# A mixture-of-experts layer after an attention: gates worked out chunk by chunk during the attention, tokens gathered without their layernorm, first expert weights fetched early

## The chip, the cores and the metric

The kernel runs on one core of a Trainium2 chip, as one launch. The metric is the device time in microseconds, taken as the median of several runs. Five engines work side by side, each through its own queue of instructions in order: TensorE (PE, with its weight loads shown as PEld), VectorE (DVE), ScalarE (ACT), GpSimd (POOL) and SyncE (SP), which only issues the transfers. They wait for each other through semaphores.

## What is computed

The input is two images of 56 x 56 tokens (L = 3136) with 128 channels. Four layers follow one another: two state-space layers with convolutions, one layer of attention and a long-convolution mixer, and a last layer of attention and experts. The change lies in the last layer:

```python
t = t + _L3_attn_ref(_ln_t(t), ...)      # softmax attention over all 3136 tokens, per image
t = t + _L3_ffn_ref(_ln_t(t), ...)       # experts

def _ln_t(v, eps=1e-5):                  # per token, over its 128 channels
    return (v - mean(v)) / sqrt(var(v) + eps)

def _L3_ffn_ref(x, gate_w, gate_b, weight1, weight2):     # E = 64 experts, K = 8
    logits = x @ gate_w.T + gate_b                         # [b, 3136, 64]
    probs = softmax(logits, axis=1)                        # over the tokens
    vals, idx = top_k(probs.transpose(0, 2, 1), K)         # each expert takes its 8 best tokens
    pooled[b, e] = sum_k vals[b, e, k] * x[b, idx[b, e, k]]
    h = gelu(pooled[b, e] @ weight1[e, :128] + weight1[e, 128])
    o = h @ weight2[e, :512] + weight2[e, 512]
    out[b, idx[b, e, k]] += vals[b, e, k] * o[b, e]
```

All arithmetic that matters here is in fp32. Each expert has 128 x 512 and 512 x 128 weights, 0.5 MB together, 33.5 MB for 64 experts, which are read from DRAM once.

## The kernel before

The kernel is written in a tile framework: pools give out buffers in on-chip memory, the framework derives waits from who reads and writes which buffer, and a scheduler lays each engine's instructions in an order that may differ a little from the order in the program.

**Tokens.** `k.X` holds the residual stream, [112, 28, 2, 128]: 28 tiles of 112 tokens, two images, 128 channels. Seven chunks (NCH) of 448 tokens make up an image.

**Attention 3** (`Attention3.run`, `Attend.run`). Keys of the first image are prepared, then 14 chunks of 448 queries run, seven per image. In each, 25 steps j go over 128 keys: a product `sc` on PE (L1031), Exp on ACT (L1033), a running sum `total` on POOL (L1042, L1044), and, two steps later, the product `av` (L1025). Beside that, up to j = 15 of every chunk but the last, `Queries.some` forms a bound for the next chunk's scores: two bf16 products `lo` a step (L966) and a maximum of each on DVE (L970). `lo` has two banks of PSUM, `sc` three, `pr` one. At the end of a chunk the result is normalised and added to X (L1060 to L1070). A hook `also(at, j)` is called after each step; in chunks 0 to 3 it prepares the second image's keys: at j = 1 and 13 `tokens` (four transposes L1202, sum into X L1203, layernorm), at j = 6 and 18 `channels` (four transposes L1216), at j = 9 and 21 `key_tiles` (L1227). The layernorm of a chunk (`layernorm_tokens`) is L77, L78, L79 on DVE, the squares L80 on ACT, their sum L81 on DVE, the square root L82 on ACT, its reciprocal L83 on DVE and the multiplication L84 on POOL. Square root and Exp need different function tables on ACT, so each layernorm brings two ACT_TABLE_LOADs.

**Experts** (`layer3_experts`, after attention 3 has ended and its memory is free). First SP issues the loads of the gate's weights and of the first four groups of experts (a group is four experts: 1 MB of `w1` and four pieces of 256 KB of `w2`, whose rows in one partition are 512 bytes long). Then:

- layernorm of all tokens, in four pieces of 14 x 128 columns (L79 to L84), into U
- transposes of U to `uT` (L108, 56 of them, copies L64 and L68), then the gates `pr` [128, 3136], with 64 experts of image 0 above 64 of image 1: two accumulated products per chunk (L1695), bias on ACT (L1699)
- softmax over the 3136 columns and the top 8: L1701 to L1709, each over the whole of `pr`. `sel` is then the probability where it is among the top 8, else 0
- `sel` is transposed to tokens (L1714) and each image's 28 tiles of U are multiplied by it, so that `pooled` holds the weighted sums (`pp`, L1719; copies L1724)
- the loop over 16 groups: `ph` (L1747) multiplies `pooled` by `w1` for four experts; a copy, four transposes `pt` (L1758), the bias `b1` and Gelu follow; `every` (L1738) multiplies by `w2` of the group before. A group's buffers are refilled as they come free; `w1` and `w2` are separate tiles, four of each
- `oe` times `sel` gives the output's addition (L1787), X is added (L1792), and the result is stored

Of the kernel before, what the change touches and what calls it, by code (L numbers as in the profile page):

```python
# [70 lines left out]
def layernorm_tokens(k, out, x, sq, st, d):  # L71


    nc = k.nc
    g = x.shape[1]
    mean, var = st[:, 0, :], st[:, 1, :]
    nc.vector.tensor_reduce(mean, x, AX.X, ALU.add)  # L77
    nc.vector.tensor_scalar_mul(mean, mean, 1.0 / d)  # L78
    nc.vector.tensor_tensor(out, x, mean.unsqueeze(2).to_broadcast([TP, g, d]), ALU.subtract)  # L79
    nc.scalar.activation(sq, out, AF.Square)  # L80
    nc.vector.tensor_reduce(var, sq, AX.X, ALU.add)  # L81
    nc.scalar.activation(var, var, AF.Sqrt, bias=k.eps[:TP], scale=1.0 / d)  # L82
    nc.vector.reciprocal(var, var)  # L83
    nc.gpsimd.tensor_tensor(out, out, var.unsqueeze(2).to_broadcast([TP, g, d]), ALU.mult)  # L84


def layernorm_all(k, U):

    with k.tc.tile_pool(name="lnp", bufs=2) as pool:
        for j in range(0, NT, 7):  # L90
            sq = pool.tile([TP, 14, C], F32, name="sq")
            st = pool.tile([TP, 2, 14], F32, name="st")
            layernorm_tokens(
                k,
                U[:, j : j + 7, :, 0:C].rearrange("p j b c -> p (j b) c"),
                k.X[:, j : j + 7].rearrange("p j b c -> p (j b) c"),
                sq, st, C,
            )
# [1024 lines left out]
class Attention3:  # L1123
# [35 lines left out]
    def run(self, A):  # L1159

        k = self.k
        with ExitStack() as ctx:
            kp = ctx.enter_context(k.pool("a3"))
            self.uT = [kp.tile([128, L], F32, name=f"u{b}") for b in range(B)]
            self.low = [kp.tile([128, L], BF16, name=f"low{b}") for b in range(B)]
            self.V = [kp.tile([KT, NKT, C], F32, name=f"V{b}") for b in range(B)]
# [13 lines left out]
            def also(at, j):  # L1180

                half, part = divmod(j, 12)
# [10 lines left out]
            att.run(self.uT, queries, self.V, 1.0 / 16, self.Wv, also=also)  # L1193

# [463 lines left out]
def layer3_experts(k, d, out):  # L1658
# [5 lines left out]
    nc, tc, X = k.nc, k.tc, k.X  # L1664
    NE, NH, EC = 64, 512, 4
    with ExitStack() as ctx:
        sp = ctx.enter_context(tc.tile_pool(name="e3", bufs=1))
        W = {n: load(nc, sp, d["L3_" + n], "L3" + n) for n in ("gate_w", "gate_b", "b1", "b2")}
        wp = ctx.enter_context(tc.tile_pool(name="e3w", bufs=4))
        weights = {}  # L1670

        def fetch(e0):
            w1 = wp.tile([128, EC, NH], F32, name="w1")
            w2 = wp.tile([128, EC, 4, C], F32, name="w2")
            nc.sync.dma_start(w1, d["L3_weight1"][e0 : e0 + EC, 0:C].rearrange("e d h -> d e h"))
            for e in range(EC):
                nc.sync.dma_start(w2[:, e], d["L3_weight2"][e0 + e, 0:NH].rearrange("(c p) o -> p c o", p=128))
            weights[e0] = w1, w2

        for e0 in range(0, 4 * EC, EC):  # L1680
            fetch(e0)
        pr = sp.tile([128, L], F32, name="pr")
        sel = sp.tile([128, L], F32, name="sel")
        pooled = sp.tile([128, NE, 2 * EC], F32, name="pooled")
        nc.gpsimd.memset(pooled, 0.0)
        with tc.tile_pool(name="e3u", bufs=1) as up, tc.tile_pool(name="pe3", bufs=2, space=PSUM) as pp:
            U = up.tile([TP, NT, B, C], F32, name="U")
            layernorm_all(k, U)
            uT = up.tile([128, B, L], F32, name="uT")
            for b in range(B):  # L1690
                tokens_to_channels(k, pp, lambda c0: uT[:, b, c0 : c0 + CH], lambda j: U[:, j, b, :])
            for c in range(NCH):
                ps = pp.tile([128, CH], F32, name="pt")
                for b in range(B):
                    nc.tensor.matmul(  # L1695
                        ps, lhsT=W["gate_w"][:, b, :], rhs=uT[:, b, CH * c : CH * (c + 1)],
                        start=b == 0, stop=b == 1,
                    )
                nc.scalar.activation(pr[:, CH * c : CH * (c + 1)], ps, AF.Identity, bias=W["gate_b"])  # L1699
            m = sp.tile([128, 8], F32, name="m")  # L1700
            nc.vector.tensor_reduce(m[:, 0:1], pr, AX.X, ALU.max, negate=True)  # L1701
            nc.scalar.activation(pr, pr, AF.Exp, bias=m[:, 0:1])
            nc.vector.tensor_reduce(m[:, 1:2], pr, AX.X, ALU.add)
            nc.vector.reciprocal(m[:, 1:2], m[:, 1:2])
            nc.vector.tensor_scalar(pr, pr, m[:, 1:2], None, ALU.mult)
            top = sp.tile([128, 8], F32, name="top")
            nc.vector.max(top, pr)
            nc.vector.match_replace(sel, top, pr, -1.0)
            nc.vector.scalar_tensor_tensor(sel, sel, 0.0, pr, ALU.is_lt, ALU.mult)  # L1709
            selT = up.tile([TP, NT, 128], F32, name="selT")  # L1710
            for j in range(0, NT, 4):
                ps = pp.tile([TP, 4, 128], F32, name="ps")
                for i in range(4):
                    nc.tensor.transpose(ps[:, i, :], sel[:, TP * (j + i) : TP * (j + i + 1)], k.ident)  # L1714
                k.evacuate(selT[:, j : j + 4, :], ps)
            for b in range(B):
                ps = pp.tile([128, NE], F32, name="pp")
                for j in range(NT):
                    nc.tensor.matmul(  # L1719
                        ps, lhsT=U[:, j, b, :], rhs=selT[:, j, NE * b : NE * (b + 1)],  # L1720
                        start=j == 0, stop=j == NT - 1,
                    )
                for e in range(EC):
                    nc.vector.tensor_copy(pooled[:, e::EC, 2 * e + b], ps[:, e::EC])  # L1724
        with tc.tile_pool(name="e3h", bufs=2) as hp, tc.tile_pool(name="pex", bufs=2, space=PSUM) as pp, tc.tile_pool(
            name="poe", bufs=1, space=PSUM
        ) as po:
# [3 lines left out]
            every = po.tile([128, C], F32, name="every")  # L1731
            ready = None

            def second(e0, w2, t):
                for e in range(EC):
                    z = NE - 1 - (e0 + e)
                    for c in range(4):
                        nc.tensor.matmul(  # L1738
                            every, lhsT=t[:, e, c, z : z + 128], rhs=w2[:, e, c, :],
# [3 lines left out]
            for e0 in range(0, NE, EC):  # L1743
                w1, w2 = weights.pop(e0)
                ph = pp.tile([2 * EC, NH], F32, name="ph")
                for e in range(EC):
                    nc.tensor.matmul(  # L1747
                        ph, lhsT=pooled[:, e0 + e, :], rhs=w1[:, e, :], start=e == 0, stop=e == EC - 1
                    )
                hr = hp.tile([2 * EC, NH], F32, name="hr")  # L1750
                nc.vector.tensor_copy(hr, ph)
                if ready is not None:
                    second(*ready)
                    if ready[0] + 4 * EC < NE:
                        fetch(ready[0] + 4 * EC)
                pt = pp.tile([128, 4, EC, B], F32, name="pt")
                for c in range(4):
                    nc.tensor.transpose(  # L1758
                        pt[:, c].rearrange("p e b -> p (e b)"), hr[:, 128 * c : 128 * (c + 1)],
                        k.ident[: 2 * EC, : 2 * EC],  # L1760
# [169 lines left out]
```

## Time and profile before

| what | us |
|---|---|
| median of 5 runs | 9354.45 (9341.42 to 9356.66) |
| profiled execution | 9343.85 |
| its span, first to last instruction | 9341.7 |
| attention 3, of the span | about 8370 to 9100 |
| experts, of the span | about 9100 to 9341.7 |

Busy over the whole span: PE 8138.4 (87%), DVE 7101.5 (76%), POOL 6327.4 (68%), ACT 3856.2 (41%). The granted PE clock is 0.949 in the mean.

A row of the profile that groups instructions names the line, the engine, the operation and the tiles (out<-in), then the count, and its busy time or the mean time of one. The chain of work that ended last is followed back from the end, from each instruction to what released it; "issue" is time for which the profile shows no cause. Rows that begin with numbers are times in us from the start of the span. PE's products in fp32 take two passes, so each appears twice.

### The profile page before, as it was taken

What the parts mean: (1) busy time and instruction counts of PE and PEld (TensorE: products, weight loads), DVE (VectorE), ACT (ScalarE), POOL (GpSimd) and SP (SyncE); (2) the same over time, 40 slices, a digit from 0 to 9 for tenths busy, and PEclk for the clock granted to TensorE, in tenths of its full rate; (3) what the DMA queues carried; (4) which work ended last, traced back from release to release, by engine and by line L of the source; (5) the groups of instructions that cost most, each with busy time, mean ns of one, the idle gap of its engine ahead of it and who ended that gap; (6) DMA issues with size and microseconds to landing.
All of it is one profiled execution on the core that took longest, in us unless ns stands there. A gap on an engine that the chain in (4) does not pass through costs nothing.

```text
span 9341.7 us, 94244 instructions
## 1 busy us (share of the span) xinstructions
PE 8138.4 (87%) x28823; PEld 4793.0 (51%) x28823; DVE 7101.5 (76%) x7517; ACT 3856.2 (41%) x6560; POOL 6327.4 (68%) x4013
## 2 busy tenths in 40 slices
PE   7888888888888888888888888599999999999997
PEld 3444445444444444444444444355588888875545
DVE  8999998999996997998899799711366766665432
ACT  4555545555545555555555555333211111114331
POOL 5999996999994996998899699666411111115550
PEclk9999999999998998999999899699999999999998
DMA  5666664666663884886687488200233333310005
GB/s 155 221 221 214 215 205 132 221 221 214 213 213 95 224 216 122 221 218 166 179 222 214 124 221 215 71 3 4 64 105 95 105 102 99 99 53 1 1 10 150
DMA packets 798151, 1364.60 MB, mean 146 GB/s; under 512 B 125278, under 2 KB 431455, under 8 KB 797611
## 3 DMA queue, kind: packets, MB, share of 16 engines
q1 hardware_dynamic: 797642, 1358.56, 50.1%
q8 instruction: 229, 3.75, 0.2%
q14 instruction: 280, 2.29, 0.1%
HBM read 1318.63 MB, written 39.60 MB: 145 GB/s over the span
## 4 chain that ended last, share of the span: by engine, by line
PE 49%; DVE 21%; issue 12%; ACT 9%; POOL 4%; DMA 3%; SPq 1%; DVEq 0%; POOLq 0%; ACTq 0%
PE cv L1501 12%; DVE h L351 10%; PE acc L371 7%; DVE h L410 7%; PE av L1025 6%; PE sc L1031 6%; PE pj L1615 4%; ACT a L332 3%; PE b L175 3%; PE acc L385 2%; POOL p L423 1%; PE pcv L452 1%; DMA whole<-rows 1%; PE b L357 1%; DMA c<-rows 1%
## 5 line engine op out<-in xcount | busy, mean ns | idle before, releaser
L423 POOL TENSOR_TENSOR p<-h,c 128x784 f32<-128x784 f32 x2048 | 3763.1, 1861 | 235.3 <-PE acc L371 151.1
L371 PE MATMUL acc<-p,ident 128*128 128x392 f32 x8192 | 3144.8, 515 | 84.8 <-POOL p L423 80.7
L351 DVE TENSOR_TENSOR_SCAN h<-a,state,h 128x784 f32<-128x784 f32 x1536 | 2796.9, 1840 | 86.7 <-ACT a L332 63.6
L371 PEld LDWEIGHTS acc<-p,ident 128*128 128x128 f32 x8192 | 1524.1, 198 | 1180.8 <-POOL p L423 193.4
L410 DVE TENSOR_TENSOR h<-du,b 128x784 f32<-128x784 f32 x1408 | 1334.5, 948 | 182.6 <-PE b L357 180.5
L332 ACT ACTIVATE a<-delta,L0A 128x784 f32<-128x784 f32 x1024 | 938.8, 918 | 839.0 <-DVE h L351 837.2
L426 POOL TENSOR_TENSOR h<-du,b 128x784 f32<-128x784 f32 x640 | 1188.8, 1858 | 3.1 <-DMA b<-rows 3.1
L357 PE MATMUL b<-three,sel 96*128 96x512 bf16 (+1 forms) x2816 | 709.5, 333 | 542.5 <-DVE h L410 499.7
L332 ACT ACTIVATE a<-delta,L1A 128x784 f32<-128x784 f32 x1024 | 936.7, 917 | 538.8 <-DVE h L351 536.5
L1044 POOL TENSOR_TENSOR total<-total,e 128x448 f32<-128x448 f32 (+1 forms) x644 | 731.4, 1136 | 345.0 <-ACT e L1033 308.8
L351 DVE TENSOR_TENSOR_SCAN h<-a,h 128x784 f32<-128x784 f32 x512 | 901.8, 1779 | 41.2 <-ACT a L332 23.5
L1514 DVE TENSOR_TENSOR u<-u,cv 128x512 f32<-128x512 f32 x1024 | 623.6, 680 | 327.0 <-PE cv L1501 325.7
L357 PEld LDWEIGHTS <-sel 96*128 96x128 bf16 x2816 | 276.4, 98 | 1154.8 <-issue 913.6
L1545 POOL TENSOR_TENSOR u<-u,S 128x1024 f32<-128x1024 f32 x64 | 150.1, 2366 | 1045.0 <-DVE S L1514 1045.0
L1033 ACT ACTIVATE e<-sc 128x448 f32<-128x448 f32 (+1 forms) x700 | 377.4, 543 | 770.5 <-PE sc L1031 580.3
L1516 ACT COPY u<-cv 128x512 f32<-128x512 f32 x256 | 149.3, 586 | 827.2 <-PE cv L1501 773.6
L1615 PE MATMUL pj<-u,Wm 128*128 128x196 f32 (+8 forms) x1536 | 352.6, 383 | 5.7 <-DVE A L1621 5.7
L1031 PE MATMUL sc<-big 128*128 128x448 f32 (+1 forms) x700 | 324.0, 549 | 12.2 <-ACT e L1033 12.2
L1025 PE MATMUL av<-e,big 128*128 128x448 f32 (+1 forms) x700 | 322.4, 548 | 1.1 <-DVE e L1038 1.0
L1031 PE MATMUL sc<-q,u 128*128 128x448 f32 (+1 forms) x700 | 323.0, 546 | 0.3 <-DVE q L984 0.3
L1025 PE MATMUL av<-e,V 128*128 128x448 f32 (+1 forms) x700 | 320.9, 545 | 0.0
L970 DVE TENSOR_REDUCE m<-lo 112x1 f32<-112x448 f32 x392 | 227.3, 618 | 118.4 <-PE lo L966 118.1
(415 smaller groups left out, 10454.9 us busy)
## 6 DMA issues: line engine op xcount, KB each, us to landing
c<-rows SPq DMA_DIRECT2D x1024, 392.0 KB, 3.9
c<-rows SPq DMA_DIRECT2D x2048, 196.0 KB, 4.4
b<-rows SPq DMA_DIRECT2D x320, 392.0 KB, 4.5
b<-rows SPq DMA_DIRECT2D x640, 196.0 KB, 4.5
H<-raw SPq DMA_DIRECT2D x32, 1568.0 KB, 7.4
wC<-win SPq DMA_DIRECT2D x64, 576.0 KB, 6.3
wA<-win SPq DMA_DIRECT2D x64, 384.0 KB, 5.4
wD<-win SPq DMA_DIRECT2D x64, 320.0 KB, 4.3
```

Source lines behind the costliest of these rows:

```text
L332: self.k.nc.scalar.activation(x["a"], g["delta"][ci], AF.Exp, scale=self.w["A"](g["kd"], ci, x["n"]))
L351: self.k.nc.vector.tensor_tensor_scan(h, a, h, start, ALU.mult, ALU.add)
L357: self.k.nc.tensor.matmul(ps[:, c0:c1], lhsT=self.w["selB"](x["n"]), rhs=x["g"]["three"][:, c0:c1], start=True, stop=True)
L371: nc.tensor.matmul(job["acc"][:, i, 0:392], lhsT=self.k.ident, rhs=x["p"][:, 392 * i : 392 * (i + 1)], start=False, stop=n == NS - 1,)
L410: nc.vector.tensor_tensor(one["h"], one["g"]["du"][one["ci"]], one["b"], ALU.mult)
L423: nc.gpsimd.tensor_tensor(now["p"], now["h"], now["c"], ALU.mult)
L426: nc.gpsimd.tensor_tensor(three["h"], three["g"]["du"][three["ci"]], three["b"], ALU.mult)
L1025: nc.tensor.matmul(acc, lhsT=V[b][:n, j, :], rhs=e[:n], start=j == 0, stop=j == NKT - 1)
L1031: nc.tensor.matmul(ps[:n], lhsT=keys[b][:, KT * j : KT * j + n], rhs=q, start=True, stop=True)
L1044: nc.gpsimd.tensor_tensor(total[:n], total[:n], e[:n], ALU.add)
L1501: self.k.nc.tensor.matmul(ps[:, b], lhsT=v[:, C * b : C * (b + 1)], rhs=h, start=i == 0, stop=i == len(terms) - 1)
L1615: nc.tensor.matmul(ps[:, lo - c0 : hi - c0], lhsT=Ws[f][:, eo, r, :], rhs=u[:, b, f, lo - a0 : hi - a0], start=f == 0, stop=f == 1,)
```

## The change

The experts become a class `Experts`, which is built before attention 3 and is handed to it.

- For each chunk of 448 tokens of an image, one chunk after it has been attended to, the hook now calls `experts.tokens` at j = 3 (layernorm of that chunk, keeping the reciprocal deviation in `by`) and `experts.gates` at j = 8 (four transposes, a copy, one gate product, the bias, and the chunk's own eight largest logits into `tops`). The last chunk's are done after the attention. That is 14 times a set.
- The eight largest of an expert's row come from its 56 candidates in `tops`, and `match_replace` runs on the logits in place of the probabilities. The sum of the Exps comes from the Exp's own accumulator, and the scaling by its reciprocal goes from DVE to ACT.
- The gathering multiplies raw X instead of U: the transposed `sel` is multiplied by `by` (so DVE drains all of these banks), and the mean is taken off afterwards by one product with `less`, which is the identity minus 1/128. Eight copies to `pooled` alternate between DVE and ACT.
- Weights come in pairs of experts, each pair in one tile of 8 KB per partition, with one transfer for `w1` and one for `w2`, all with 2 KB rows; for that, hidden units are dealt to partitions as `(p c)`. `b1` is loaded straight from the weights with the same deal. The first six pairs are put into A (the mixer's output) and `first` (keys and values of the first image) as soon as the attention has finished with them, seven more pairs into a pool after the attention, and from then on two pairs at a time once a group has been used up. The program places `fetch_first` in chunk 8; the order of SP's queue has it waiting on the readers of A and `first`.

```diff
-def layernorm_tokens(k, out, x, sq, st, d):
+def layernorm_tokens(k, out, x, sq, st, d, by=None):
...
-    mean, var = st[:, 0, :], st[:, 1, :]
+    mean, var = st[:, 0, :], st[:, 1, :] if by is None else by
...
-    def run(self, A):
+    def run(self, A, experts):
...
-            self.uT = [kp.tile([128, L], F32, name=f"u{b}") for b in range(B)]
+            self.uT = [experts.first[:, 0:L], kp.tile([128, L], F32, name="u1")]
...
             def also(at, j):
+                if at > 0 and j == 3:
+                    experts.tokens(self.sp, *divmod(at - 1, NCH))
+                elif at > 0 and j == 8:
+                    experts.gates(self.sp, lambda: att.bank("pr"), *divmod(at - 1, NCH))
+                elif at == NCH + 1 and j == 0:
+                    experts.fetch_first(A)
...
             att.run(self.uT, queries, self.V, 1.0 / 16, self.Wv, also=also)
+            experts.tokens(self.sp, B - 1, NCH - 1)
+            experts.gates(self.sp, lambda: att.bank("pr"), B - 1, NCH - 1)
...
+class Experts:
+    PAIR = 2 * (512 + 512)
+    def __init__(self, k, ctx, d):
+        ...
+        self.b1 = sp.tile([128, self.NE, 4], F32, name="b1")
+        nc.sync.dma_start(self.b1, d["L3_weight1"][:, C].rearrange("e (p c) -> p e c", c=4))
+        self.first = sp.tile([128, L + NKT * C], F32, name="first")
+        self.pr = sp.tile([128, L], F32, name="pr")
+        self.by = sp.tile([TP, NT, B], F32, name="by3")
+        self.tops = sp.tile([128, NCH, 8], F32, name="tops")
+    def tokens(self, pool, b, c):
+        js = slice(4 * c, 4 * (c + 1))
+        self.U = pool.tile([TP, 4, C], F32, name="U")
+        ...
+        layernorm_tokens(self.k, self.U, self.k.X[:, js, b, :], sq, st, C, by=self.by[:, js, b])
+    def gates(self, pool, bank, b, c):
+        ...
+        ps = bank()[:, 0:CH]
+        for i in range(4):
+            nc.tensor.transpose(ps[:, TP * i : TP * (i + 1)], self.U[:, i, :], k.ident[:TP, :TP])
+        uT = pool.tile([128, CH], F32, name="ug")
+        nc.vector.tensor_copy(uT, ps)
+        ps = bank()[:, 0:CH]
+        nc.tensor.matmul(ps, lhsT=self.W["gate_w"][:, b, :], rhs=uT, start=True, stop=True)
+        nc.scalar.activation(self.pr[rows, cs], ps[rows], AF.Identity, bias=self.W["gate_b"][rows])
+        nc.vector.max(self.tops[rows, c], self.pr[rows, cs])
+    def fetch(self, w):
+        ...
+        nc.sync.dma_start(w1, d["L3_weight1"][e : e + 2, 0:C].rearrange("e d h -> d e h"))
+        nc.sync.dma_start(w2, d["L3_weight2"][e : e + 2, 0 : self.NH].rearrange("e (p c) o -> p e c o", c=4))
+    def fetch_first(self, A):
+        A = A.rearrange("p b t -> p (b t)")
+        for t in (A, self.first):
+            for i in range(3):
+                self.fetch(t[:, self.PAIR * i : self.PAIR * (i + 1)])
+    def run(self, out):
+            ...
+            wp = ctx.enter_context(k.pool("e3w", 7))
+            for i in range(7):
+                fetch()
+                nc.vector.max(top, self.tops.rearrange("p c n -> p (c n)"))
+                nc.vector.tensor_scalar_mul(m[:, 0:1], top[:, 0:1], -1.0)
+                nc.vector.match_replace(sel, top, pr, -3e38)
+                nc.scalar.activation(pr, pr, AF.Exp, bias=m[:, 0:1], accum_out=m[:, 1:2])
+                nc.vector.reciprocal(m[:, 2:3], m[:, 1:2])
+                nc.scalar.activation(pr, pr, AF.Copy, scale=m[:, 2:3])
+                nc.vector.scalar_tensor_tensor(sel, sel, -2e38, pr, ALU.is_lt, ALU.mult)
+                    ...
+                    nc.vector.tensor_tensor(selT[:, j : j + 4], ps, by, ALU.mult)
+                        ...
+                            ps[:, b], lhsT=X[:, j, b, :], rhs=selT[:, j, b], start=j == 0, stop=j == NT - 1
+                nc.vector.tensor_copy(raw, ps)
+                nc.tensor.matmul(ps, lhsT=less, rhs=raw, start=True, stop=True)
+                for b in range(B):
+                    for e in range(EC):
+                        k.evacuate(pooled[:, e::EC, 2 * e + b], ps[:, b, e::EC])
...
                 if ready is not None:
                     second(*ready)
-                    if ready[0] + 4 * EC < NE:
-                        fetch(ready[0] + 4 * EC)
+                    if ready[0] >= 12:
+                        fetch()
+                        fetch()
...
-                        pt[:, c].rearrange("p e b -> p (e b)"), hr[:, 128 * c : 128 * (c + 1)],
+                        pt[:, c].rearrange("p e b -> p (e b)"), hr[:, c::4], k.ident[: 2 * EC, : 2 * EC]
```

## Prediction, made before the changed kernel had run

> **What bounds the kernel now.** I read the page first (PE 87% busy, DVE 76%), then the chain of work that ended last, and from it only the part the change reaches: attention of layer 3 (8370 to 9100 us) and the experts (9100 to 9342). In program order the two kernels issue the same instructions on every engine up to attention 3, so 0 to 8370 us costs the same. Next came busy time by stage: columns are busy us of PE, PE's weight loads, DVE, ACT, POOL, then PE's granted clock, DMA share, GB/s.
>
> ```profile
> core 0: us, PE busy (x) PEld busy (x) DVE busy (x) ACT busy (x) POOL busy (x), PEclk, DMA share, GB/s
> ...
> 8774.00:8821.00 47.00, 47.00 (x152) 24.16 (x151) 18.91 (x36) 14.73 (x27) 27.11 (x24) 1.00 0.00 1
> ...
> 9100.00:9192.00 92.00, 40.50 (x224) 31.38 (x225) 48.15 (x47) 23.40 (x28) 12.98 (x5) 0.67 0.32 95
> 9192.00:9317.00 125.00, 124.19 (x705) 73.96 (x705) 17.20 (x81) 6.77 (x33) 4.91 (x2) 0.99 0.67 202
> 9317.00:9342.00 25.00, 19.59 (x114) 18.32 (x112) 9.92 (x15) 0.00 (x0) 0.00 (x0) 0.66 0.50 129
> ```
>
> In an attention chunk, PE has no idle time: what is added to PE there is added to the end. In the 92 us from attention to the first expert, PE is busy 40 at clock 0.67: a chain of other engines sets the pace. The loop of 16 expert groups is PE's again (124.2 of 125). The chain says what the 92 us are (start, us, engine, tile, line):
>
> ```profile
> 9099.37 1.14 DVE X L1070 x4
> ...
> 9100.60 3.96 DVE U L79 x2
> ...
> 9126.17 6.33 POOL U L84 x2
> ...
> 9139.52 10.80 PE pt L1695 x28
> ...
> 9151.02 3.43 DVE m L1701
> ...
> 9173.42 3.84 PE ps L1714 x16
> ...
> 9180.55 10.90 PE pp L1719 x98
> 9191.46 0.56 issue
> 9192.01 5.23 PE ph L1747 x8
> ```
>
> Layernorm of both sequences (9100.6 to 9132.5), transposes and gates on PE to 9150.3, softmax and top 8 over 3136 columns on DVE and ACT to 9173.4, then transposes of `sel` and the gathering on PE. The transfers in the tail, in 40 slices of 6.55 us from 9080:
>
> ```profile
> GB/s 0 1 0 236 335 331 330 98 0 0 0 0 0 0 0 3 0 0 252 246 290 264 283 285 254 285 263 286 288 283 240 177 163 0 0 3 69 180 140 105
> ...
> w<-in_L_weight_dram SPq DMA_DIRECT2D x16, 1024.0 KB, 6.7
> ```
>
> The first four groups (8.4 MB) land at 330 GB/s by 9132, long before the loop. In the loop the queue runs at the 274 GB/s that PE's pace of 7.64 us per group asks for, and PE waits for no transfer.
>
> **What leaves the tail.** Sums are made against this execution (span 9341.7, time 9343.85). From the last update of X (ends 9100.50) to the first `ph` (9192.01) it takes 91.5 us.
>
> Afterwards only chunk (1,6) is left to normalise, by the rows of 112x512: L77 0.69, L78 0.17, L79 0.68, L80 0.63, table load 1.28 (starts when L80 ends, so it covers L81), square root 0.30, L83 0.18, POOL 1.04, eight hand-overs at 0.06 (the chain's "issue" pieces between engines are 0.02 to 0.07): 5.5. Then four transposes at half clock (0.24 each in the `ps` row above: 3.84/16) 1.0; copy 0.62; the gate's two passes of 448 columns at half clock 1.5 (`ph` there takes 0.86 for 512); Identity 0.63; MAX8 over 448 columns 0.55 (L1707 takes 3.43 for 3136); maximum of the maxima and negation 0.3; hand-overs 0.4: 5.0. Then match_replace 3.5, Exp 2.91, reciprocal 0.17, scaling 2.91 (moved from DVE's 1.86 to ACT, which takes Exp's time), L1709's form 3.43, hand-overs 0.3: 13.2. The Exp writes `pr` in place, so it waits for match_replace, and its table load carries that wait: 1.28 more. Sum 25.0, against 72.9 (9100.5 to 9173.4): 47.9 less. The two full reductions (L1701, L1703) and the full MAX8 are gone, the sums riding on Exp.
>
> From there to the end of `pp` (18.0 us) I keep the time: the same 28 transposes and 56 products. DVE alone now drains `ps` (0.69 per bank against PE's 0.96). New behind it: a copy of 128x128 0.28, one product 0.33, eight copies to `pooled` that now alternate between DVE (0.18) and ACT (0.2, from ACT's 16-element rows) and wait on each other, since their tile is interleaved, 4 x (0.18+0.2+0.1) = 1.9, and hand-overs 0.2: 2.7 in place of the 0.56 "issue" above: 2.1 more. **Tail: 47.9 - 2.1 = 45.8 us less.**
>
> Here a rule of the Trainium skill matters ("TensorE: Matmul & The Clock Gate", What's actually happening): PE falls to half clock after about 3.4 us of idleness. The gap before `ph` is 0.56 us, yet by the windows PE ran 9192 to 9196 at clock 0.59, so the first `ph` took 5.23 and not 3.53. By the rule the new gap of 2.7 us would find PE warm (1.7 less); by the row it starts cold as before. I take the row: 0.
>
> **What enters attention.** For 13 chunks, during the next chunk: five DVE steps of layernorm, L80 and L82 on ACT with two table loads, L84 on POOL; four transposes, the copy `ug`, the gate product, Identity, MAX8. Nearest rows: chunks 1 to 3 already carry such sets for the second sequence (two a chunk), beside a chunk that has none:
>
> ```profile
> 8509.31:8561.46 52.15, 50.57 (x180) 26.80 (x180) 26.88 (x51) 22.87 (x38) 32.83 (x31) 1.00 0.00 1
> ...
> 8707.08:8754.67 47.59, 47.59 (x157) 24.76 (x157) 19.31 (x37) 14.72 (x27) 27.09 (x25) 1.00 0.00 0
> ```
>
> Two sets cost 52.15 - 47.58 = 4.57: 1.58 idle on PE and 2.99 of work for 23 transposes, 0.13 each. Where the idle time comes from stands in the timeline of that chunk (start, us, engine, line; in brackets idle before and its releaser):
>
> ```profile
> 8533.85 1.05 DVE L78 TENSOR_SCALAR st<-st 112x4 f32<-112x4 f32 x1
> ...
> 8535.48 0.35 PE L966 MATMUL lo<-low,q 128*112 128x448 bf16 x1 [0.45 <-DVE m L970]
> ...
> 8537.99 1.28 ACT L82 ACT_TABLE_LOAD   x1
> ...
> 8539.28 0.30 ACT L82 ACTIVATE st<-st,eps 112x4 f32<-112x4 f32 x1
> ...
> 8539.60 1.28 ACT L1033 ACT_TABLE_LOAD   x1
> ...
> 8541.03 0.60 PE L1216 MATMUL pr<-ident,U 112*128 112x112 f32 x4 [0.69 <-POOL U L84]
> ```
>
> DVE holds `lo`'s two banks 0.45 too long while it does L77 and L78 (1.05 instead of 0.17: POOL is in L1044 then), and the transposes wait 0.69 for POOL's U. The second set shows just one 0.45.
>
> Chunks 4 to 12 (nine): work 4 x 0.13 + 0.75 (a 448-column product, as L1031's pitch) = 1.27; the 0.45. U is asked for five steps of 1.88 us after L77 and is ready after some 8.5, so no wait there; `ug` has an `sc` and a `lo` product ahead of the gate (0.94) to hide behind. 9 x 1.72 = 15.5. Chunk 13 has no `lo`: 1.3. Chunks 1 to 3: the new set follows two steps behind the old one. Laying both into the old timeline, DVE's third pair of maxima ends 2.2 late, and ACT switches tables twice in a row; the later of both costs PE some 1.8: 3 x (1.27 + 1.8) = 9.3. **Attention: 26.1 us more** (16.5 if all waits are hidden; 42.5 if each chunk idles 2.0).
>
> The skill speaks against this part: "ScalarE: Activation LUTs", What ACT_TABLE_LOAD costs, puts a switch at 1283 ns and a 1380 ns drain, 2.66 us. Here the load takes 1.28 and the square root starts 0.01 later, so no drain is on the path. By the row ACT is held 3.4 us (two loads, root, one Exp), that is 1.5 beyond its step of 1.88, and `av` leaves about 2.2 before it wants that `e`. By the page it is 6.2, a lag of 4.3, so 2.1 lost per chunk. I take the row.
>
> **What costs nothing.** Six pairs fetched into A and `first` move 6.3 MB while the queue is at 1 GB/s. SP has nothing else queued there; by its order they go out as A's and `first`'s last readers finish. `b1` arrives in 8192 pieces of 16 bytes. No row here shows that; the queue is idle for some 200 us before A comes free, and should it take all of them nobody waits: 0. Without that cover it would stand ahead of these fetches. Seven pairs follow at attention's end (7.3 MB, 22 us at 330 GB/s, used 50 us later). Refills start later and w1 is freed only with w2, so the lead shrinks to about 11 us for 0.5 MB (landing now 6.7 for 1 MB). Loop and output stay at 149.7.
>
> **Sum.** 26.1 - 45.8 = -19.7: 9324.2 for this execution. The median of the runs, 9354.45, lies 10.6 above it: 9334.8, told as 9335.
>
> **Rivals.**
> 1. All hidden, a chance of 0.24: PE pays 16.5 alone. For it: copy and Identity have cover by the order; chunks without sets have DVE busy only 19.3 of 47.6. Against: even one set a chunk shows 0.45. 9325.
> 2. Queues collide, 0.14: each chunk idles 2.0 as tables, maxima and POOL line up; for it, chunk 1 to 3's double sets; against, DVE has 0.7 us free in each step. 45.8 - 42.5 = 3.3 less: 9351.
> 3. Slower, 0.05: ACT's table switches at the page's price. Nine chunks at 1.27 + 0.45 + 2.1 (34.4), chunk 13 at 3.8 (its step is 1.5, not 1.88), three at 3.1 and four drains (8.6, together 25.8), the tail's two loads 2.8: 66.8 against 45.8, 21 slower, 9375. It turns from gain to loss at 3.5 us per chunk (45.8/13). Against it: the 0.01 above.
> 4. Refills late, 0.05: ten groups each 0.7 longer (2.1 MB at 250 GB/s, as the loop's lowest slices read, rather than 274): 9342. Against: 330 GB/s at the start, with pieces of w2 that were then 512 bytes.
>
> **Numbers.** My own case has 0.52 and spans 9329 to 9341. Faster or slower is told from no change by 0.2%, 18.7 us here, so the bound is 9335.7 and my case lies just under it: I give six tenths of it to faster (0.31) and the rest to no change. With rival 1 faster is 0.55, rounded up to 0.56 for the part of rival 2's mild end; no change 0.39; slower 0.05. The range: down to rival 1 with PE's clock a window better (9321), up to rival 2 (9350); rival 3 is outside.
>
> **What would show it.** First `ph` should start 45 to 46 us after the last X update; chunk periods of 49.3 (4 to 12), and about 55 (1 to 2), against 47.6 and 52.15; 16 groups still at 7.64 without a DMA releaser before `ph`; table loads 1.28 with the next ACT row right behind. Wrong if a period above 50.5 shows `e` or `m` as PE's releaser, if the scheduler's order leaves the gate waiting on `ug`, or if the transposes of `sel` warm up late.

## The result, and the profile after

The changed kernel takes 9332.28 us, median of 22 runs (9312.63 to 9347.83), the kernel before 9352.1 (40 runs, 9336.22 to 9362.36): a ratio of 0.998, 95% interval 0.9974 to 0.9986. That is 19.8 us less. The profiled execution took 9336.75 us with a span of 9335.0.

Its span is only 6.7 us below that of before, although the medians differ by 19.8. The reason lies ahead of the change: the last long group of the mixer's products (`pj`, 128x271) starts at 8359.63 in the profiled execution of before and at 8369.44 in that of after, in code that is the same. Over the fourteen profiled executions of this study that start lies between 8358.5 and 8372.9. So stages are compared by their own lengths, from that group on:

| stage (us) | before | after | change | predicted |
|---|---|---|---|---|
| last `pj` group to the first shift (`mm`) | 63.0 | 63.9 | +0.9 | 0 |
| chunk 0 | 34.4 | 36.7 | +2.3 | 0 |
| chunks 1 to 3 | 154.8 | 161.7 | +7.0 | +9.3 |
| chunks 4 to 12 | 428.2 | 442.95 | +14.7 | +15.5 |
| chunk 13 to the last X update | 60.4 | 61.6 | +1.2 | +1.3 |
| tail, to the first `ph` | 91.5 | 45.9 | -45.6 | -45.8 |
| loop, to the first `po` | 125.5 | 130.3 | +4.8 | 0 |
| output | 24.2 | 22.5 | -1.7 | 0 |
| sum | 982.1 | 965.6 | -16.5 | -19.7 |

Chunk 0 is no effect of the change: over the fourteen executions it took either 34.4 to 34.8 or 36.7, six and eight of them, and the kernel of the run late_fetch, which issues the same there, had 34.57. PE's granted clock reads 0.98 in that stretch of before and 0.90 in that of after. Nor is the output's 1.7: the fourteen executions took 22.5 to 25.0 us for it, and hr_dealt, whose output code is that of the changed kernel, took 25.0. PE's clock falls to 0.50 in the middle of that stage, about 7.5 us in before and 12 us in after.

Busy time by stage after, columns as in the prediction: a chunk with sets of both kinds, a chunk of the second half, the tail, the loop.

```profile
core 0: us, PE busy (x) PEld busy (x) DVE busy (x) ACT busy (x) POOL busy (x), PEclk, DMA share, GB/s
8470.09:8524.57 54.48, 52.48 (x186) 27.31 (x186) 31.34 (x58) 26.78 (x43) 33.92 (x32) 1.00 0.03 10
8828.70:8877.91 49.21, 49.03 (x162) 25.39 (x163) 23.18 (x44) 18.85 (x32) 28.49 (x26) 1.00 0.00 1
9136.30:9182.20 45.90, 21.91 (x149) 19.40 (x149) 16.71 (x24) 10.47 (x11) 3.07 (x2) 0.65 0.37 136
9182.20:9312.48 130.28, 129.18 (x705) 77.75 (x706) 17.77 (x83) 6.96 (x35) 3.22 (x2) 0.98 0.44 154
```

Attention is still PE's alone, 49.03 of 49.21 us. DVE's busy time in a chunk grew from 19.3 to 23.2 and ACT's from 14.7 to 18.9, beside PE; only PE's own growth and short waits reach the end. The tail is still a chain (PE 21.9 of 45.9, clock 0.65):

```profile
9135.17 1.14 DVE X L1056 x4
...
9147.09 3.41 DVE sel L1739
...
9150.56 1.28 ACT L1740
...
9151.86 3.01 ACT pr L1740 x2
...
9155.09 2.92 ACT pr L1742
...
9158.03 3.44 DVE sel L1743
...
9161.51 3.84 PE ps L1748 x16
...
9169.17 10.90 PE pp L1756 x98
...
9180.94 1.25 issue
9182.20 7.32 PE ph L1788 x10
```

From the X update to match_replace are 10.8 us for one chunk, where the chain of before needed 49.8 for both sequences' layernorm, transposes and gates (9100.5 to 9150.3). Then four passes over 3136 columns follow one another, each waiting for the one before, and the table load of 1.28 between them.

In the timeline of a chunk of the second half (start, us, engine, line, tile; in brackets idle before and its releaser) a set's parts stand among attention's:

```profile
8854.18 0.35 PE L952 MATMUL lo<-low,q 128*112 128x448 bf16 x1 [0.18 <-DVE m L956]
...
8854.36 1.28 ACT L82 ACT_TABLE_LOAD   x1
...
8855.65 0.30 ACT L82 ACTIVATE by<-by,eps 112x4 f32<-112x4 f32 x1
...
8862.64 0.55 PE L1693 MATMUL pr<-ident,U 112*128 112x112 f32 x4
...
8863.99 0.94 PE L1697 MATMUL pr<-ug,L3gate_w 128*128 128x448 f32 x2
```

PE's steps are 1.88 us apart in this chunk where nothing intervenes. Read by the starts of its instructions, the set adds 0.39 for the transposes, 0.78 for the gate product and 0.46 where `lo` comes late because DVE's maxima stand behind L78 and L79: 1.63, the period's growth of 1.64. Only 0.18 of the 0.46 is called idle; the rest hides in the overlap of pipelined products. The table load takes 1.28 and the root starts 0.01 after it.

### The profile page after: what moved, and what is told of

It reads as the page before. It is cut to its first block, busy times and chain, and to the rows that moved or that the text cites. A ratio compares the mean times of both kernels' runs of the same rounds, so it can differ in the third digit from the quotient of the medians.

```text
span 9335.0 us, 94373 instructions
## 1 busy us (share of the span) xinstructions
PE 8149.5 (87%) x28825; PEld 4797.1 (51%) x28825; DVE 7118.3 (76%) x7587; ACT 3895.5 (42%) x6609; POOL 6331.8 (68%) x4023
## 4 chain that ended last, share of the span: by engine, by line
PE 50%; DVE 21%; issue 12%; ACT 9%; POOL 4%; DMA 3%; SPq 1%; DVEq 0%; POOLq 0%; ACTq 0%
PE cv L1499 12%; DVE h L337 10%; PE acc L357 8%; DVE h L396 7%; PE av L1011 5%; PE sc L1017 5%; PE pj L1613 4%; ACT a L318 3%; PE b L161 3%; PE acc L371 2%; PE pcv L438 1%; POOL p L409 1%; DMA c<-rows 1%; PE b L343 1%; DMA whole<-rows 1%
## 5 line engine op out<-in xcount | busy, mean ns | idle before, releaser
L1017 PE MATMUL sc<-big 128*128 128x448 f32 (+1 forms) x700 | 324.1, 549 | 12.1 <-ACT e L1019 12.1
L187 ACT CAST bands<-whole 128x196 bf16<-128x196 f32 x270 | 95.8, 355 | 528.6 <-POOL whole L190 272.2
L1593 POOL TENSOR_TENSOR both<-mpm 128x512 f32<-128x512 f32 x32 | 40.6, 1270 | 390.4 <-DVE Wm L1649 271.7
L1613 PEld LDWEIGHTS pj<-u,Wm 128*128 128x128 f32 x1536 | 268.5, 192 | 71.3 <-issue 46.0
```

Of the source, the lines that this page charges most:

```text
L1017: nc.tensor.matmul(ps[:n], lhsT=keys[b][:, KT * j : KT * j + n], rhs=q, start=True, stop=True)
L1613: nc.tensor.matmul(ps[:, lo - c0 : hi - c0], lhsT=Ws[f][:, eo, r, :], rhs=u[:, b, f, lo - a0 : hi - a0], start=f == 0, stop=f == 1,)
```

## The experiments

My theory was the prediction's own: the gain is work moved from a chain into PE-bound chunks. The rivals: the early fetch carries part of it; the tail's steps became cheaper; switches of ACT's table cost more than their row. Beside these stood the unpredicted growth of the loop. Stage lengths below come from each run's profiled execution. Differences of a few us are read from them alone: of all the ratios below, only those of sets_after and pieces_wide have an interval clear of the changed kernel's (0.9974 to 0.9986).

**late_fetch**: the fetch is issued behind the last gate.

```
-                elif at == NCH + 1 and j == 0:
-                    experts.fetch_first(A)
...
             experts.gates(self.sp, lambda: att.bank("pr"), B - 1, NCH - 1)
+            experts.fetch_first(A)
```

> The six early pairs are fetched when the last gate has been issued instead of during attention 3, into the same tiles; nothing else is changed. My theory (the early fetch is worth nothing by itself): all 13 pairs, 13.6 MB, go out from about the last update of X on and at 330 GB/s have landed 41 us later, before the first ph asks for its pair, so the tail stays at 45.9 us, the groups at 7.87, the chunk periods at 49.22, and the time is that of the changed kernel within 0.05%. Rival (the early fetch carries part of the gain): the first ph or the loop waits for a DMA, tail or loop 5 to 30 us longer, the ratio to the kernel before 0.9985 to 1.001. Third case (the fetch disturbs attention): chunk periods fall below 49.1.

9336.35 us, ratio 0.9981 (0.9975 to 0.9988), beside the changed kernel's 0.998. Tail 45.92, groups 7.87, periods 49.22. The early fetch is worth nothing here, and costs nothing. In after's own trace the fetches trickle out from 8381.7 to 8793 as the regions of A and `first` come free.

**sets_after**: all sets behind attention, a set's layernorm issued ahead of the gate of the set before.

```
-                if at > 0 and j == 3:
-                    experts.tokens(self.sp, *divmod(at - 1, NCH))
-                elif at > 0 and j == 8:
-                    experts.gates(self.sp, lambda: att.bank("pr"), *divmod(at - 1, NCH))
...
+            for i in range(2 * NCH + 1):
+                if i < 2 * NCH:
+                    experts.tokens(self.sp, *todo[i])
...
+                    experts.gates(self.sp, lambda: att.bank("pr"), *todo[i - 1])
```

> All 14 sets of layernorm, transposes and gates run after attention 3 instead of 13 of them beside it (a set's layernorm is issued ahead of the gate of the set before, so that they overlap). The softmax by chunk maxima, the divisors in the gates and the early fetch stay. My theory (the gain is the place, not a smaller sum of work): chunk periods go back to 47.58 (second half) and 52.15 (chunks 1 and 2), attention 22 to 25 us shorter; each of the 13 sets costs about 7.4 us of chained steps in the tail (five DVE rows and two waits for ACT, copy, cold gate product 1.87, Identity, maximum), so the tail is about 142 us (110 to 150) where the kernel before has 91.5, and the time about 50 us above the kernel before (ratio 1.002 to 1.007). Rival (the tail is short because its steps became cheaper: no reductions over 3136 columns, no second sequence to normalise, raw tokens gathered): the tail stays below 91 and the kernel is still faster than before.

9358.74 us, ratio 1.0009 (1.0001 to 1.0018): the gain is gone. Its attention chunk and its tail:

```profile
8700.00:8747.58 47.58, 47.58 (x157) 24.74 (x156) 19.31 (x37) 14.75 (x27) 27.38 (x25) 1.00 0.04 12
9099.07:9195.87 96.80, 58.44 (x226) 34.03 (x227) 55.95 (x102) 28.20 (x46) 14.81 (x13) 0.57 0.18 65
```

PE's 47.58 are back, and the tail takes 96.8, more than the 91.5 of before, though it has the chunk maxima, the fewer passes and the divisors in the gates. The tail splits where the last gate's bias ends on ACT:

| tail (us) | before | after | sets_after |
|---|---|---|---|
| last X update to the end of the last gate | 50.5 | 9.7 | 61.0 |
| from there to the first `ph` | 41.0 | 36.2 | 35.8 |

So the rival has a part: the steps behind the gates are about 5 us shorter wherever the sets stand. The other 40.8 of the 45.6 are the place, and with the place taken back the whole gain is gone, for set after set in a row takes 10.5 longer than the layernorm of all tokens did before. My size was off: I had 7.4 us per exposed set, the gate products are 4.37 apart, since a set's layernorm runs beside the gate before it. The 13 sets cost 50.9 us in the tail, where the changed kernel pays 22.0 for them in attention (666.3 against 644.3 from chunk 1 to the last X update).

**no_switch**: no root, so no table switch, in the experts' layernorm.

```
+    root = AF.Sqrt if by is None else AF.Identity
-    nc.scalar.activation(var, var, AF.Sqrt, bias=k.eps[:TP], scale=1.0 / d)
+    nc.scalar.activation(var, var, root, bias=k.eps[:TP], scale=1.0 / d)
```

> In the experts' layernorm alone the square root is replaced by an Identity with the same scale and bias, so that ACT keeps the table of the exponential; this leaves the root out of those divisors and changes the gates. My theory (the switches are off the path beside attention): periods in the second half stay at 49.22 (at least 49.04, which is PE's busy time), chunks 1 and 2 come down from 54.48 by at most 0.9, the tail loses its two loads, 2.5 us, so the time is 2.5 to 5 us below the changed kernel. Rival (a switch costs more than its 1.28 row shows, by a drain, and attention pays for it): second-half periods fall to 48.9 or lower, chunks 1 and 2 by 2 or more, 8 us or more in all.

9332.05 us, ratio 0.9979 (0.9973 to 0.9986). Second-half periods stay at 49.22 with ACT 2.5 us less busy (16.31 for 18.85), chunks 1 and 2 fall by 0.32 to 54.15, the tail by 1.8 to 44.1 (I had 2.5). Beside attention the switches are hidden but for some 1 us in chunks 1 to 3; a price beyond the row would have shown in the second half.

**hr_dealt**: the loop's transposes read neighbouring columns again.

```
-                nc.vector.tensor_copy(hr, ph)
+                nc.vector.tensor_copy(hr.rearrange("q (c p) -> q c p", c=4), ph.rearrange("q (p c) -> q c p", c=4))
...
-                        pt[:, c].rearrange("p e b -> p (e b)"), hr[:, c::4], k.ident[: 2 * EC, : 2 * EC]
+                        pt[:, c].rearrange("p e b -> p (e b)"), hr[:, 128 * c : 128 * (c + 1)], k.ident[: 2 * EC, : 2 * EC]
```

> The hidden units are dealt to the four transposes by the DVE copy from ph to hr (read with a stride of four, written in order), so the transposes of the loop read 128 neighbouring columns again; the weights stay as the changed kernel has them. My theory (the weight load of a transpose with a stride of 16 bytes takes 0.14 for 0.08): the four loads of pt fall from 0.55 to 0.32, a group from 7.87 to 7.64, 16 groups save 3.7 us, and the DVE copy of 0.68 stays hidden behind the 3.8 us of products even if it doubles. Rival (the 0.23 comes from the weights, now in pairs and in A, first and w): pt falls but the group stays at 7.87, or neither falls.

9324.59 us, ratio 0.9971 (0.996 to 0.9982). Weight loads by group (line, engine, shapes, count, busy us, mean ns) in some 100 us of the loop, after:

```profile
L1798 PEld LDWEIGHTS pt<-ident,hr 8*128 8x128 f32 x56 | 7.7, 207 | 1.7
```

and with the units dealt by the copy:

```profile
L1798 PEld LDWEIGHTS pt<-ident,hr 8*128 8x128 f32 x52 | 4.2, 137 | 1.6
```

Before, the same row reads 136 ns. A stride of four costs 70 ns a load here and, with it, PE its time: the group falls from 7.87 to 7.64, the loop from 130.28 to 126.60, that is by 3.7. DVE's copy takes 0.68 in both, with or without the stride.

**exp_apart**: Exp is written to a tile of its own.

```
-                nc.scalar.activation(pr, pr, AF.Exp, bias=m[:, 0:1], accum_out=m[:, 1:2])
+                ex = up.tile([128, L], F32, name="ex")
+                nc.scalar.activation(ex, pr, AF.Exp, bias=m[:, 0:1], accum_out=m[:, 1:2])
...
-                nc.scalar.activation(pr, pr, AF.Copy, scale=m[:, 2:3])
-                nc.vector.scalar_tensor_tensor(sel, sel, -2e38, pr, ALU.is_lt, ALU.mult)
+                nc.scalar.activation(ex, ex, AF.Copy, scale=m[:, 2:3])
+                nc.vector.scalar_tensor_tensor(sel, sel, -2e38, ex, ALU.is_lt, ALU.mult)
```

> The exponential is written to a tile of its own instead of over the gates, so that it need not wait for match_replace, which reads them. My theory (the in-place write costs what the prediction charged, one match_replace and one table load): the table load follows the last Identity, Exp runs beside match_replace (3.41 us) and ends about when it ends, scaling follows, and the tail falls by 4.5 us, from 45.9 to 41.4 (41.0 to 42.0). Rival (DVE and ACT slow each other down over the same 3136 columns, or the table load still comes late): the tail falls by under 2 us. Chunk periods and the loop stay.

9329.03 us, ratio 0.9978 (0.9971 to 0.9985); tail 42.5, 3.4 less where I had 4.5. Its timeline:

```profile
9147.17 3.41 DVE L1739 MATCH_REPLACE8 sel<-top,pr 128x3136 f32<-128x3136 f32 x1
9147.27 1.28 ACT L1741 ACT_TABLE_LOAD   x1 [1.18 <-DVE m L1738]
...
9148.56 2.91 ACT L1741 ACTIVATE ex<-pr,m 128x3136 f32<-128x3136 f32 x1
```

The two do run side by side at their old durations, but ACT sat idle for 1.18 before the table load, until `m`, Exp's bias, was there: the load, which reads no `m`, was held for what the activation behind it needs. That is about the missing 1.1.

**gate_later**: the gate product two steps behind its transposes and copy (`gates` split in two, called at j = 8 and j = 10).

> In attention the gate product is issued two steps after the transposes and the copy ug, instead of right behind them. Theory (0.19 of the 1.46 us that a set adds to PE in a chunk of the second half is the gate's weight load waiting 0.36 for ug): those periods fall from 49.22 to 49.03 (48.95 to 49.08), nine of them by 1.7 us. Rival (the 1.46 are work: a product with new weights of its own costs more than its 448 columns): 49.22 stays. The other idle time of 0.18 (lo waiting for DVE's maxima while DVE does L77 and L78) stays by both.

9334.19 us, ratio 0.9983 (0.9975 to 0.999). The periods are 49.19: 0.03 of the expected 0.19. My theory fell; the set's PE cost is work (0.40 and 0.75 by the starts) and the 0.46 of the maxima, which stay. The tail of 44.7 and the loop of 129.1 in this execution are not the edit's: PE's clock rose 2.5 us earlier in the transposes of `sel` and fell only 1.0 us into the first `ph` (rows under "The clock rule").

**warm_before, warm_gap, gap_filled**: useless products on PE. Shown are the 14 of warm_before; warm_gap issues one such product behind the product with `less`, and gap_filled four of 128 columns there, on `raw`.

```
+                wm = pp.tile([128, 512], F32, name="wm")
+                for i in range(14):
+                    nc.tensor.matmul(wm, lhsT=k.ident[:TP], rhs=X[:, 0:2].rearrange("p j b c -> p (j b c)"), start=True, stop=True)
```

> 14 products of no use (512 columns, 0.88 us each at full clock) are issued on PE between the last gate product and the transposes of sel, where PE has been idle for 16 us. Theory (PE's half clock after the gap is on the path): the transposes of sel run at 0.15 instead of 0.24 us each from the first on, and the tail falls from 45.9 to 44.2 or lower; the first ph is still at half clock. Rival (DVE's seven multiplications of 0.69 and the 11 us of products behind them set the pace): tail 45.4 to 46.2.

> One product of no use (512 columns, 0.88 us at full clock) is issued on PE right behind the product with less, into the 1.27 us in which PE waits for the copies to pooled ahead of the first ph. Theory A (the short idle gap itself lowers the clock): the product and the first ph run at full clock, the first ph takes 3.6 us instead of 6.5, and from first ph to output it takes 127.4 us instead of 130.28. Theory B (the clock was already lowered for what came before, so filling the gap comes too late): the product takes 1.76 at half clock, ph starts up to 0.6 later and is at half clock as well, 130 us or more from there; PE's granted clock reads 0.50 in the 4 us after it.

> The changed kernel with four products of 128 columns on raw (0.9 us together at full clock) right behind the product with less, ahead of the first ph; made to depend on raw, since the useless product of the earlier run was issued 45 us before that gap. Theory A (the idle gap of 1.27 us lowers the clock): these products and the first ph run at full clock, 127.4 us from first ph to output for 130.28. Theory B (the clock is lowered all the same, by what came before or at a moment of its own): ph is at half clock for 3 to 6 us, 129 us or more. A single look: a warm ph alone would not prove A, since one of nine runs had it without this.

The first did not test what I had meant, since the order of the program put the products elsewhere. Timeline of warm_before:

```profile
9136.57 7.11 PE L1737 MATMUL wm<-X,ident 112*128 112x512 f32 x16
...
9162.07 3.84 PE L1753 MATMUL ps<-ident,sel 128*112 128x128 f32 x16 [11.89 <-DVE sel L1748]
```

They ran from the last X update on; the last gate then took 0.60 and 1.02 instead of 1.01 and 1.86, and the tail 43.6, but the transposes of `sel` were cold as before. Yet here the first `ph` was at full clock, behind the same gap of 1.2 us, and the loop took 127.4. 9332.54 us, ratio 0.9979 (0.997 to 0.9988). In warm_gap the product went out 46 us before the gap: tail 45.90 and loop 130.26, nothing tested (9329.99 us, ratio 0.9975, 0.9965 to 0.9984). In gap_filled the products stood in the gap, and the first `ph` was at full clock (loop 127.4; a single run, 9337.99 us). With warm_before beside it, that does not prove that the gap sets the clock; it stays open.

**tail_in_pieces, tail_pieces_warm**: the tail pipelined over seven pieces; the second with ten useless products ahead.

```
-                nc.vector.match_replace(sel, top, pr, -3e38)
-                nc.scalar.activation(pr, pr, AF.Exp, bias=m[:, 0:1], accum_out=m[:, 1:2])
-                nc.scalar.activation(pr, pr, AF.Copy, scale=m[:, 2:3])
-                nc.vector.scalar_tensor_tensor(sel, sel, -2e38, pr, ALU.is_lt, ALU.mult)
+                for c in range(NCH):
+                    nc.scalar.activation(ex[:, cs], pr[:, cs], AF.Exp, bias=m[:, 0:1], accum_out=sums[:, c : c + 1])
+                    nc.vector.scalar_tensor_tensor(sel[:, cs], pr[:, cs], top[:, 7:8], ex[:, cs], ALU.is_ge, ALU.mult)
+                    ps = turn(4 * c)
+                    if turned is not None:
+                        divide(*turned)
+                        gather(turned[0])
+                    turned = 4 * c, ps
...
+                    nc.vector.tensor_tensor(raw[:, b], both[b], share[:, b], ALU.mult)
...
+            nc.vector.scalar_tensor_tensor(oe, every, m[:, 2:3], oe, ALU.mult, ALU.add)
```

> What the runs so far point to, together: softmax, selection, transposes and gathering go in seven pieces of 448 columns, so that ACT, DVE and PE work on neighbouring pieces at once; Exp is written apart; the eight largest are kept by comparing with the eighth maximum instead of match_replace (an exact tie would keep a ninth); 1/sum is applied to the gathered 128x128 and to the experts' outputs instead of to 3136 columns; pooled is filled by two strided copies instead of eight; the hidden units are dealt by the copy to hr. Attention and the early fetch stay. My theory (the tail is a chain of whole-row steps that can overlap): with the maxima known 10.8 us after the last X update as now, the first piece reaches PE 1.7 later, seven pieces of four transposes and eight products at 2.5 us make 17.5, and 2 us lead to ph: tail 32 us (29 to 36) for 45.9; groups 7.64; in all 16 to 20 us below the changed kernel, ratio to the kernel before 0.9955 to 0.9968. Rival (DVE's queue sets the pace, since it must take turns between selecting and dividing, and PE stays at half clock): tail 37 to 44, ratio above 0.9970.

> The kernel of the run beside it, with ten products of no use on PE (512 columns) from the last X update on. Theory (half clock is on the path of the last gate and of the pieces): the last gate's transposes and product are 1.3 us shorter, as they were with 14 such products, pieces of PE's work take 2.0 instead of 2.5 us, and the tail is 3 to 5 us shorter than the run beside it. Rival (DVE and ACT set the pace): 1.3 us or less.

9329.91 us, ratio 0.9972 (0.9961 to 0.9983), and 9328.42, 0.9968 (0.9956 to 0.9981). (`turn` is the four transposes of a piece, `divide` its multiplication by the divisors, `gather` its eight products.) The tails are 45.0 and 43.8: my theories missed. Of the first run's rival only the half clock came true, for DVE waits for PE and not the other way. The second run's rival has the right size, 1.2, all of it from the last gate. 30 us of tail_in_pieces, from the first piece on:

```profile
9152.24:9162.00 9.76, 9.76 (x46) 9.39 (x47) 5.52 (x9) 3.15 (x10) 0.00 (x0) 0.50 0.97 359
9162.00:9182.00 20.00, 20.00 (x97) 20.00 (x96) 5.65 (x7) 0.00 (x0) 2.66 (x1) 0.50 0.00 0
```

PE is busy without a gap, and its clock never leaves 0.50; a piece takes 4.16 instead of 2.5. In the changed kernel the gathering products ran at 1.00, in one unbroken stretch behind the transposes (10.90 for 98 of them).

**pieces_wide**: the same, with the gathering products streaming 128 columns instead of 64.

```
-                                both[b], lhsT=X[:, i, b, :], rhs=selT[:, i, b], start=i == 0, stop=i == NT - 1
+                                both[b], lhsT=X[:, i, b, :], rhs=selT[:, i], start=i == 0, stop=i == NT - 1
...
-                    nc.vector.tensor_tensor(raw[:, b], both[b], share[:, b], ALU.mult)
+                    nc.vector.tensor_tensor(raw[:, b], both[b][:, b], share[:, b], ALU.mult)
```

> As tail_in_pieces, but each gathering product streams both sequences' 128 columns of selT instead of 64 (the other sequence's half of the result is not used), so PE has twice the columns per weight load. In tail_in_pieces PE was busy without a gap for 30 us at a granted clock of 0.50. Theory (what counts for the clock is how much the array is used, and 64 columns behind each load of 128x128 weights are too few to raise it): the clock comes back to 1.00 within 4 to 9 us of the first piece; at full clock a product costs what its weight load costs (0.12 for 0.11), so a piece falls from 4.16 to 2.5 us and the tail from 45.0 to 32 to 37 us; ratio to the kernel before 0.9955 to 0.9970. Rival (the clock was held down by something else, as the interleaving with transposes or a phase of its own): the clock stays at 0.50, a piece takes 4.3 or more, tail 45 to 47.

9307.17 us, ratio 0.9948 (0.9935 to 0.9962), the fastest kernel of this study and faster than I had forecast. Its windows, from the first piece on:

```profile
9148.88:9152.00 3.12, 3.12 (x13) 2.75 (x14) 3.12 (x6) 3.12 (x10) 0.00 (x0) 0.50 1.04 398
9152.00:9154.00 2.00, 2.00 (x12) 2.00 (x11) 1.78 (x4) 0.03 (x1) 0.07 (x1) 0.53 1.05 391
9154.00:9160.00 6.00, 6.00 (x56) 6.00 (x56) 3.23 (x5) 0.00 (x0) 2.59 (x1) 1.00 0.67 245
```

The clock is back after 5 us, a piece falls to 2.2 and the tail to 33.0, and the first `ph` is at full clock too (loop 123.8). Twice the columns cost less time, because 16 products take 3.52 at half clock with either width, and 1.95 at full clock.

## Why the prediction was right, and where it was not

**Time and sign.** 9335 was forecast and 9332.3 measured. The mechanism holds: sets_after takes the place back and loses the gain. In the profiled pair the steps sum to 16.5 less, not 19.7, and 3.1 of that difference are the stretch before chunk 1, where the changed kernel had the worse clock. That the medians differ by 19.8 is closer to the forecast than its terms deserve: some of them erred in opposite directions, as follows.

**The tail** was right in its sum and in its parts: 25.2 us to the end of `sel` (25.0 predicted), 18.6 from there to the end of `pp` (18.0), 2.1 to `ph` (2.7). Of the price put on the in-place Exp, one match_replace and one table load, exp_apart won back 3.4 and not 4.5. Of the 45.6 some 5 are cheaper steps behind the gates, and the rest is the place.

**Attention** was oversized by 3.2 of 26.1, most of it in the term for chunks 1 to 3 (3.1 each; 2.3 measured). There the later of two delays, DVE's maxima or the doubled table loads, was to cost PE some 1.8 beyond its 1.27 of work (three times that is 9.2, told as 9.3); 1.05 is left for it in the measured 2.3, and without the new set's two loads a chunk is only 0.32 shorter. The rows of one set were right: 0.39 for 0.52, 0.78 for 0.75, 0.46 for 0.45. Rival 1 falls, since the maxima do wait; rival 2 falls, since the idle time beyond PE's work is 0.46 and not 2.0.

**Table switches.** The row was right against the page's price ("ScalarE: Activation LUTs", What ACT_TABLE_LOAD costs): no drain of 1.38 lies between load and root, and taking the switches out of the second half changes 49.22 by nothing. Rival 3 is refuted by that run.

**Fetches**: 0 was right by late_fetch, and no transfer releases PE in the loop, so rival 4 falls as well. The 16-byte pieces of `b1` went out at 8340.3, in the mixer's end, and took the queue about 5 us (DMA share 1.03 from 8340 to 8345); the prediction had them in front of A, with some 200 us of cover; the first fetch into A went out at 8381.7, 41 us later, and that was cover enough.

**"Loop and output stay at 149.7"** is the step that failed: the loop grew by 4.8. The prediction followed the weights' new deal as far as the queue and not into the transposes, whose `hr[:, c::4]` is a weight operand. That term is 16 x 0.23 = 3.7, by hr_dealt. The other 1.1 are the first `ph`: half clock was rightly taken from the row, but lasted 5.8 us for 3.3. That the sum came out near all the same is luck: the attention term's excess of 3.2 and the output's 1.7, which is the clock's and not the change's, together cover this miss.

**The clock rule.** By the page "TensorE: Matmul & The Clock Gate" (What's actually happening) an idle window of about 3.4 us lowers the clock and a busy one of that length raises it. The row was the better guide: after gaps of 1.3 us the first `ph` ran at half clock in after, late_fetch, sets_after, no_switch, hr_dealt, exp_apart and warm_gap, and 30 busy us in tail_in_pieces, and as many in tail_pieces_warm, did not raise it. pieces_wide shows that the width of the products decides there, for the edit changes nothing else of PE's work; whether columns count per weight load or per time is not separated. Why the clock falls around the first `ph` stays open. The gap just before it is not needed for that: in sets_after the clock fell at about 9193.75, before the product with `less` and 2.1 us ahead of `ph`, and in gate_later it was still 1.00 through the gap and fell 1.0 us after `ph` had begun at 9179.49 (PE alone: us, busy, clock):

```profile
9178.50:9179.50 1.00, 0.01 (x1) 1.00 0.00 0
9179.50:9180.50 1.00, 1.00 (x3) 1.00 0.00 0
9180.50:9181.50 1.00, 1.00 (x3) 0.52 0.00 0
```

That the narrow products before it are the reason was only argued.

## What to carry to other kernels

Work in a serial chain between two PE-bound stages is worth moving into the stage before even when PE pays for part of it: 50.9 us of chain became 22.0 beside attention. Moving the transfers early gave nothing, and the 5 us from trimming the chain's later steps went back in the 4.8 by which the loop grew. When a layout is changed for a transfer's sake, follow it to every operand that reads it, weight loads of transposes included. Before pipelining a PE stage, read its granted clock: in this tail overlap alone won 0.9 us at a clock of 0.50, and wider products 12.1 more.

## What was not expected of the hardware

- PE stayed at a granted clock of 0.50 through 30 us of unbroken products of 64 columns and transposes (tail_in_pieces), and rose to 1.00 after 5 us when the products had 128 columns (pieces_wide).
- A weight load of 8x128 with a stride of 16 bytes took 207 ns (after), 137 without (hr_dealt), while a DVE copy of 8x512 took 0.68 us in both.
- A table load was held for the inputs of the activation behind it: ACT sat idle for 1.18 us until that activation's bias was there (exp_apart).
- In tail_in_pieces DVE's copy of 128x128 (`across`) took 2.65 us, for about 0.3 for other copies of that size, and ended with POOL's memset of 2.66 us that had begun just before it (9163.78); nobody waited for it. It took 2.65 beside such a memset in tail_pieces_warm too, and in pieces_wide 1.08, again ending with the memset. Whether the memset holds it was not tested.
